# Expert results added straight into the output, and two loads and sums moved, in a four-layer graph and expert kernel

## The chip, the core and the metric

The kernel runs on one core of one Trainium2 chip. Its engines are TensorE (PE in the profile, its weight loads PEld), VectorE (DVE), ScalarE (ACT), GpSimd (POOL) and SyncE (SP). SP and ACT issue plain DMAs from their own queues, POOL issues those that use a list of indices. The metric is the device time of one execution in microseconds; the median of three runs stands for the kernel.

## The reference, cut to what matters

Input is x (625 x 1024, float32), 20,625 edges sorted by destination, with a type from 0 to 7. Four layers follow, each on the layer norm of x and added to x.

```python
# layer 1: relational graph convolution with a gate
out = x @ root + bias
for r in range(8):
    mask = (edge_type == r)
    mean = segment_sum(x[src] * mask, dst) / max(count, 1)
    out = out + mean @ weight[r]
z = concat([out, x]) @ w_gate + b_gate
h = tanh(out) * z + x * (1 - z)
# layer 2: 8-bit quantized linear layer
# layer 3: graph convolution with degree norms
# layer 4: top-2 of 8 experts, capacity 196 tokens each
combine, dispatch = _top2_gating(x @ router_w, capacity)
expert_in = einsum('nec,nh->ech', dispatch, x)
hmid = silu(einsum('ech,ehf->ecf', expert_in, w1) + b1)
expert_out = einsum('ecf,efh->ech', hmid, w2) + b2
y = einsum('nec,ech->nh', combine, expert_out)
out = y + 0.1 * (silu(x @ sw1 + sb1) @ sw2 + sb2)
```

The kernel's output is x plus the last `out`.

## The kernel before

625 rows are five tiles of 125 (`NT`). A matmul writes a PSUM tile of up to 128 x 512; four such tiles rotate (`mm_tile`). The function is built as one long program. A planner of the framework puts the instructions into each engine's queue, by its own estimate of when they can run and by the order in which they are written; at run time an engine takes its queue strictly in order. The helper `behind` asks the planner for an order without a wait, `after` adds a real wait, `in_order` chains DMAs of SP's queue, and `in_steps` and `on_pe` chain steps on TensorE.

**Units (to about 639 us).** For each relation r, `unit` (L530) multiplies the normed x with the relation's 1024 x 1024 weight, by a seven-product scheme on pairs of tiles (`tile_pair`, L452). Each recombination on VectorE is kept in `posted`; the last three of the last pair are L476, L478 and L480. Results (`ys`) go to DRAM (`yd`), except those of relation 7, which stay. Meanwhile the edges are counted in a table of DRAM (L365, L389): entry (relation, source, destination).

**Relations (about 639 to 837 us).** `order` (L580) is relation 7, then 0 to 6; I call the steps relation 0 to 7 of this stage. Each multiplies the count matrix with the unit's rows (`products`, L626), in two column halves h of five tiles t each, and adds the mean into X (L684). For exactness in the fast float format every row tile is split (`split`, L595) into an upper part `hi`, cast by ACT (L602), and the rest, by VectorE (L606). The split for the next half is written inside the loop of the present one. Also in the loop: `over_sources` (L609) sums counts over sources (L614, L616), needed by `number` (L638); `over_relations` (L619) sums counts over relations into `btot`, by an ACT copy (L622) for the first relation and VectorE additions (L624) for the rest. The area of `btot` still serves the last products of the units until they are done. Row tiles are loaded about one relation ahead (`load_y`), counts three ahead. At step `R - 3`, relation 5, SP also gets the four blocks of 1 MB of the gate's weights (L670), that `gate` reads after the loop.

**Layers 2 and 3** follow (`quantized`, `columns`, `neighbours`).

**Experts (from about 1070 us).** The router's masks give each expert a list of slots. `fill_slots` (L1155) makes `token_i`, the row of `tokens` to gather for each slot; an empty slot points to a spare row behind the 625. For the last `NL` = 4 experts there is a second list, `out_i`: in an empty slot it has a token that isn't the expert's, so that a row of zeros is added there and no spare row is needed. It comes from one-hot tiles that `find_others` (L1181, VectorE) writes and `fill_others` (L1192, TensorE) multiplies with digits of the token's number. `shared_out` (L1222) makes x + 0.1 shared in X and sends it to `total`, a DRAM area of 625 rows and the spare ones.

For expert e, `gather` brings the rows, `turn` transposes them, `expert_hidden` and `expert_out` do the two products. VectorE scales by the gate and adds the bias (L1329) into one of two `ye` buffers, and POOL adds the rows into DRAM (L1339). These scatters wait for all scatters of the expert before (`earlier`), since two experts can have a token in common. Experts 0 to 3 add to `total`. Then one DMA copies `total` to `out`:

```python
d = in_order(nc.sync.dma_start(flat_rows(out), flat_rows(total)))
after(d, [*sent, *done])
sent = [d]
```

Experts 4 to 7 add to `out`, expert 7 in halves of a row (`half_i`). The function is also written a second time, for graphs with more edges between two nodes than the fast format can hold; it is skipped here, and `exact` and `done` concern it.

Of the kernel before, what the change touches and what calls it, by code (L numbers as in the profile page):

```python
# [11 lines left out]
I32 = mybir.dt.int32  # L12
# [20 lines left out]
BEFORE = 4096.0  # L33
YB = 4 * NT
NE = 8
NL = 4
F = 256
CAP = 196
CP = CAP // 2
# [8 lines left out]
def layers(  # L48
# [163 lines left out]


    tokens = dram.tile([N + 2 * CP, D], F32, name="tokens")
    total = dram.tile([N + 2 * CP, D], F32, name="total")
    key_rows = dram.tile([ET, P], F32, name="key_rows")


# [13 lines left out]

    pe_last = None
    posted = []
    copied = []
    group = []
    counting = iter(())

# [13 lines left out]
    def weight_block(w, i, h):  # L252
        return w_chunk(wts, w, 4 * i, h * HC)
# [198 lines left out]
    def tile_pair(b, ts, put, p, between=()):  # L452
        t0, t1 = PAIRS[p]
        s1, s2, s4 = (sums[:, 3 * p + i] for i in range(3))
        steps = iter(between)

        def product(lhs, rhs):
            ps = mm_tile()
            on_pe(quarter, ps, lhs, rhs)
            for f in next(steps, ()):  # L460
                f()
            go_on()
            return ps[:P, :]
# [3 lines left out]
        copied.append(nc.scalar.copy(p1, ps))  # L467
# [12 lines left out]
        post(nc.vector.tensor_add(put(t0, 1), ps, u2))  # L480
# [98 lines left out]

    order = [R - 1, *range(R - 1)]  # L580
    counted, over, parts = {}, {}, {}

    def load_counts(r):
        counted[r] = bp.tile([P, NT, N], FR, tag="b", name="b")
# [10 lines left out]
    def split(r, h, k):  # L595

        y = held[r][k, h].bitcast(F32)
        if exact:
            parts[r, h, k] = [y]
            return  # L600
        hi = hp.tile([P, HC], F32R, tag="hi", name="hi")
        nc.scalar.copy(hi, y)  # L602
        lo = held[r][k, h]
        if r == order[0]:
            lo = yp.tile([P, HC], F32R, tag="y", name="y")
        nc.vector.tensor_sub(lo, y, hi.bitcast(F32))  # L606
        parts[r, h, k] = [lo, hi]

    def over_sources(r, k):  # L609

        v = counted[r].bitcast(F32)
        if k == 1:
            over[r] = crp.tile([P, N], FR, tag="over", name="over")
            d = nc.vector.tensor_add(over[r], v[:, 0, :], v[:, 1, :])  # L614
        else:
            d = nc.vector.tensor_add(over[r], over[r].bitcast(F32), v[:, k, :])  # L616
        behind(d, posted[-1])

    def over_relations(r, k):  # L619
        v = counted[r].bitcast(F32)[:, k, :]  # L620
        if r == order[0]:
            behind(nc.scalar.copy(btot[:, k, :], v), copied[-1])  # L622
        else:
            behind(nc.vector.tensor_add(btot[:, k, :], btot[:, k, :], v), posted[-1])  # L624

# [39 lines left out]
    firsts = [NT - 1, *range(NT - 1)]  # L665
    for k in firsts:
        split(order[0], 0, k)
    for n, r in enumerate(order):
        if n == R - 3:
            gate_w = [[weight_block(w_gate, i, h) for i in range(2)] for h in range(2)]  # L670
        for h in range(2):
            hs = slice(h * HC, (h + 1) * HC)
            for t in range(NT):
                ps = mm_tile()
# [271 lines left out]
    cleared = []  # L946
    for v in (tokens, total):
        for j in range(2):
            cleared.append(nc.scalar.dma_start(v[N + j * CP : N + (j + 1) * CP, :], zrow))

    def iota(t, pattern, base, channel):
        nc.gpsimd.iota(  # L952
# [118 lines left out]
    nc.vector.reciprocal(red, red)  # L1071
    nc.vector.tensor_mul(gates, gates, wide(red))

    NM = 2 * NE + NL
    both = mp.tile([P, NT, NM], BF16, name="masks")
    masks = both[:, :, : 2 * NE].rearrange("p t (i e) -> p t i e", i=2)
    others = both[:, :, 2 * NE :]
# [16 lines left out]
    nc.vector.tensor_add(others, masks[:, :, 0, NE - NL :], masks[:, :, 1, NE - NL :])  # L1094
    nc.vector.tensor_scalar(others, others, -1.0, 1.0, op0=ALU.mult, op1=ALU.add)


# [74 lines left out]


    aT_flat = cp.tile([P, NT * N], F32, tag="aT", name="aT")
    spots = aT_flat[:, : NL * NT * CAP // 2].bitcast(BF16)
    spots = spots.rearrange("p (e t c) -> p e t c", e=NL, t=NT)
    before = mp.tile([P, NT, NL], F32, name="before")
    out_i = mp.tile([CP, 2, NL], I32, name="out_i")
    half_i = mp.tile([CP, 2, 2], I32, name="half_i")

    def find_others():  # L1181

        nc.vector.tensor_scalar(before, others, -float(N), float(N), op0=ALU.mult, op1=ALU.add)
        nc.vector.tensor_add(before, before, pos_all[:, :NT, 2 * NE :])
        for e in range(NL):
            for t in range(NT):
                d = nc.vector.tensor_scalar(  # L1187
                    spots[:, e, t, :], io_cap, before[:, t, e : e + 1], None, op0=ALU.is_equal
                )
                behind(d, numbered[-1])  # L1190

    def fill_others(_):  # L1192
        ps = ps_sm.tile([128, HC], F32, tag="sm", name="others")
        ps = ps[:CP, : 4 * NL].rearrange("p (j e v) -> p j e v", j=2, e=NL)
        for j in range(2):
            for e in range(NL):
                for t in range(NT):
                    last = nc.tensor.matmul(
                        ps[:, j, e, :],
                        spots[:, e, t, j * CP : (j + 1) * CP],  # L1200
                        digits[:, t, :],
                        start=(t == 0),
                        stop=(t == NT - 1),
                    )
        rest_of = mp.tile([CP, 2, NL], F32, name="rest_of")
        taken_of = slots[:, :, NE - NL :, 0]
        nc.vector.tensor_scalar(rest_of, ps[:, :, :, 0], float(P), None, op0=ALU.mult)
        nc.vector.tensor_add(rest_of, rest_of, ps[:, :, :, 1])
        nc.vector.tensor_scalar(out_i, taken_of, -1.0, 1.0, op0=ALU.mult, op1=ALU.add)
        nc.vector.tensor_mul(rest_of, rest_of, out_i)  # L1210
        nc.vector.tensor_add(out_i, rest_of, slots[:, :, NE - NL :, 1])
        for h in range(2):
            nc.vector.tensor_scalar(
                half_i[:, h, :], out_i[:, :, NL - 1], 2.0, float(h), op0=ALU.mult, op1=ALU.add
            )
# [4 lines left out]
    base = []  # L1220

    def shared_out(t):  # L1222
        for h in range(2):
# [26 lines left out]
        "he": [th_flats[-1][:, c : c + 2 * CAP].rearrange("p (f c) -> p f c", f=2) for c in (0, HC)],  # L1250
    }

    def rows_at(j, e, direct=False):
        at = out_i[:, j, e - NE + NL :][:, :1] if direct else token_i[:, j, e : e + 1]
        return bass.IndirectOffsetOnAxis(ap=at, axis=0)

    def flat_rows(v):
        return v[:N, :].rearrange("n d -> (n d)").rearrange("(a b) -> a b", a=80)

    weights = {}  # L1260

# [14 lines left out]
    def gather(e):  # L1276
        for j in range(2):
            nc.gpsimd.indirect_dma_start(  # L1278
                out=rows_of_slots(e, j), out_offset=None, in_=tokens, in_offset=rows_at(j, e)
            )  # L1280

    def rows_of_slots(e, j):
        return th[2 * (e % 2) + j][:CP, :]
# [19 lines left out]
            )  # L1303
        return last

    done = sent
    sent = base + cleared

    def expert_out(e):
        nonlocal sent  # L1310
# [3 lines left out]
        for j in range(2):  # L1314
# [3 lines left out]
            for h in range(2):  # L1318
# [35 lines left out]
    for e in range(NE):  # L1354
        if 0 < e and e + 3 < NE:
            load_weights(e + 3)
        if e == 0:
            for n in range(4, NE):
                load_bias(n)
        if e == NE - NL:  # L1360
            for n in range(e + 4, NE):
                load_weights(n)
            d = in_order(nc.sync.dma_start(flat_rows(out), flat_rows(total)))
# [64 lines left out]
```

## Time and profile before

| what | before |
|---|---|
| three runs, median | 1249.19 us (1244.48 to 1249.48) |
| profiled execution, its own time | 1246.61 us |
| its span, first to last instruction | 1244.9 us |
| PE busy | 1188.5 us, 95% |
| VectorE busy | 837.9 us, 67% |
| ACT busy | 172.2 us, 14% |
| POOL busy | 487.0 us, 39% |
| mean granted TensorE clock | 0.985 |
| DMA moved | 181.72 MB, mean 146 GB/s |

The profile is of one execution. Its page gives busy times, a timeline of 40 slices, and the costliest groups of instructions with what they waited for. The trace behind it can be asked for single instructions in order of time, for who waited for whom, for the busy time of every engine in chosen stretches, and for DMA traffic. In a timeline line the columns are start, length, engine, source line, operation, output and inputs, shape and count; in brackets stand the idle time before and what released it. A line with a count above one merges instructions that follow one another. 0.3 us or less of idle time before an instruction is its issue.

### The profile page before, as it was taken

Reading aid. Unit: us, or ns where it says so; the run is one execution under the profiler, and the core shown is the slowest. Engines: PE = TensorE matmul, PEld = TensorE weight load, DVE = VectorE, ACT = ScalarE, POOL = GpSimd, SP = SyncE. Lnnn points to the kernel's source line nnn. Section 1 sums busy time; section 2 is a strip of 40 time slices with the busy share of each in tenths; the row PEclk is TensorE's granted clock in tenths of the full one; section 3 lists DMA queues with packets and bytes.
Section 4 is the critical chain, followed back from the end, with each engine's and each line's share of the span. In section 5 each row is a group of like instructions: output and inputs, shape, how many; then the busy total and the mean of one; then the engine's idle time right before and its main releaser. Section 6 shows DMA issues by size and latency. Waiting matters only on the chain. (4 is left out here: it accounts for less than half of the span.)

```text
span 1244.9 us, 11083 instructions
## 1 busy us (share of the span) xinstructions
PE 1188.5 (95%) x3810; PEld 649.8 (52%) x3810; DVE 837.9 (67%) x1340; ACT 172.2 (14%) x308; POOL 487.0 (39%) x227
## 2 busy tenths in 40 slices
PE   5999999999999999999999999899999999999992
PEld 2444444444444444444448887685445447756661
DVE  6879888888888888865149778755979416452210
ACT  1100000000000000000022122113321111313330
POOL 1005787888787888888500000004210000043312
PEclk9999999999999999999989999999999999999996
DMA  9995737373636364535455667606430025279964
GB/s 263 267 255 131 200 65 198 66 198 70 194 75 188 81 183 87 146 78 142 76 142 156 168 161 198 216 1 167 118 136 16 17 84 177 79 223 279 278 186 71
DMA packets 156288, 181.72 MB, mean 146 GB/s; under 512 B 78513, under 2 KB 95272, under 8 KB 156160
## 3 DMA queue, kind: packets, MB, share of 16 engines
q1 hardware_dynamic: 66162, 134.84, 36.7%
q0 software_dynamic: 72992, 13.31, 10.5%
q10 hardware_dynamic: 17070, 32.78, 8.6%
q8 instruction: 32, 0.52, 0.2%
q14 instruction: 32, 0.26, 0.1%
HBM read 134.22 MB, written 48.86 MB: 147 GB/s over the span
## 5 line engine op out<-in xcount | busy, mean ns | idle before, releaser
L389 POOL DMA_INDIRECT table<-hits,idx x165 | 403.8, 2447 | 199.4 <-DMA kr<-key_rows 99.7
L431 PE MATMUL mm<-w,xT 128*125 128x512 f32 x800 | 350.9, 593 | 0.0
L365 DVE SCALAR_TENSOR_TENSOR junk<-kr,key,wm 125x1375 f32<-125x1375 f32 x165 | 271.4, 1645 | 1.1
L431 PEld LDWEIGHTS mm<-w,xT 128*125 128x125 f32 x800 | 150.2, 188 | 191.7 <-issue 189.1
L629 PE MATMUL mm<-y,b 125*125 125x512 f32 x400 | 163.0, 407 | 9.1 <-DVE y L606 6.7
L629 PE MATMUL mm<-hi,b 125*125 125x512 f32 x400 | 160.5, 401 | 0.0
L431 PE MATMUL mm<-t,btot 128*125 128x512 f32 x320 | 143.8, 592 | 0.0
L1278 POOL DMA_INDIRECT th<-tokens,token_i x16 | 21.5, 1345 | 205.0 <-DVE aT L1187 172.7
L431 PEld LDWEIGHTS mm<-t,btot 128*125 128x125 f32 x320 | 60.1, 188 | 77.3 <-issue 77.3
L684 DVE SCALAR_TENSOR_TENSOR X<-mm,rc,X 125x512 f32<-125x512 f32 x80 | 59.9, 749 | 51.5 <-PE mm L629 50.4
L952 POOL IOTA io<- 125x40 f32 x1 | 0.2, 208 | 239.3 <-PE mm L629 239.3
L629 PEld LDWEIGHTS mm<-y,b 125*125 125x125 f32 x400 | 75.9, 190 | 32.2 <-DVE y L606 11.1
L629 PEld LDWEIGHTS mm<-hi,b 125*125 125x125 f32 x400 | 76.1, 190 | 18.1
L900 PE MATMUL mm<-w,xT 128*125 128x512 f32 x160 | 70.0, 595 | 2.4 <-ACT xT L187 2.4
L431 PE MATMUL mm<-w,btot 128*125 128x512 f32 x160 | 71.9, 592 | 0.0
L431 PE MATMUL mm<-t,xT 128*125 128x512 f32 x160 | 71.9, 592 | 0.0
L746 PE MATMUL mm<-w,xT 128*125 128x512 f32 x160 | 69.3, 592 | 0.0
L602 ACT CAST hi<-y 125x512 fp32r<-125x512 f32 x80 | 43.3, 617 | 147.2 <-PE mm L629 132.4
L1322 PE MATMUL mm<-w,th 128*98 128x512 f32 x128 | 56.3, 592 | 0.0
L606 DVE TENSOR_TENSOR y<-y,hi 125x512 fp32r<-125x512 f32 x80 | 53.0, 680 | 0.7 <-ACT hi L602 0.7
L450 ACT COPY y<-mm 125x512 f32<-125x512 f32 x18 | 10.5, 586 | 302.0 <-PE mm L431 291.7
L900 PEld LDWEIGHTS mm<-w,xT 128*125 128x125 f32 x160 | 29.6, 188 | 39.7 <-issue 36.0
(219 smaller groups left out, 1165.4 us busy)
## 6 DMA issues: line engine op xcount, KB each, us to landing
w<-in_L_gnn_weight_dram SPq DMA_DIRECT2D x32, 1024.0 KB
w<-in_L_ffn_w_dram SPq DMA_DIRECT2D x16, 1024.0 KB
yd<-y ACTq DMA_DIRECT2D x70, 224.0 KB
y<-yd SPq DMA_DIRECT2D x70, 224.0 KB
table<-zero SPq DMA_DIRECT2D x4, 3054.0 KB
b<-table SPq DMA_DIRECT2D x8, 1367.2 KB
kr<-key_rows ACTq DMA_DIRECT2D x15, 601.6 KB
w<-in_L_gnn_w_gate_dram SPq DMA_DIRECT2D x8, 1024.0 KB
```

Of the source, the lines that this page charges most:

```text
L365: d = nc.vector.scalar_tensor_tensor(junk, kr, key[:, c : c + 1], wm[:, (EG - 1 - j) * P : (2 * EG - 1 - j) * P], op0=ALU.is_equal, op1=AL ...
L389: d = nc.gpsimd.indirect_dma_start(out=table, out_offset=bass.IndirectOffsetOnAxis(ap=idx[:, c : c + 1], axis=0), in_=hits[:, c : c + 1], ...
L431: last = nc.tensor.matmul(ps[:P, :], lhs[:, k], rhs[:, k], start=(start and k == 0), stop=(stop and k == 3))
L450: nc.scalar.copy(put(NT - 1, h), ps[:P, :])
L602: nc.scalar.copy(hi, y)
L606: nc.vector.tensor_sub(lo, y, hi.bitcast(F32))
L629: last = nc.tensor.matmul(ps[:P, :], counted[r][:, k, t * P : (t + 1) * P], part, start=(k == ks[0] and part is parts[r, h, k][0]), stop=( ...
L684: nc.vector.scalar_tensor_tensor(X[t][:, hs], ps[:P, :], rc[:, r, t : t + 1], X[t][:, hs], op0=ALU.mult, op1=ALU.add,)
L746: last = nc.tensor.matmul(ps[:P, :], xT[:, 4 * i + k, t * P : (t + 1) * P], gate_w[h][i][:, k, :], start=(i == 0 and k == 0), stop=(i == 1 ...
L900: last = nc.tensor.matmul(ps[:P, :], xT[:, k, t * P : (t + 1) * P], gcn_w[h][k // 4][:, k % 4, :], start=(k == 0), stop=(k == KD - 1),)
L1278: nc.gpsimd.indirect_dma_start(out=rows_of_slots(e, j), out_offset=None, in_=tokens, in_offset=rows_at(j, e))
L1322: last = nc.tensor.matmul(ps[:CP, :], he[:, f, j * CP : (j + 1) * CP], weights[e][1][:, f, hs], start=(f == 0), stop=(f == 1),)
```

## The change

Four things change.

The area `total` and its copy go. `shared_out` sends x + 0.1 shared to `out`, and every expert adds there. So all eight experts need `out_i`: the masks get eight columns in place of four (`NM`), the one-hots take 40 operations and 80 products in place of 20 and 40, and their tiles lie in two areas, `aT` for six experts and the unused end of `btot` for two. `find_others` is called for two experts after each tile of `shared_out`, and `fill_others` comes after all five tiles, where it came after the second. Two clears of spare rows go as well.

The ACT copies of counts in the first relation are placed behind the cast of the tenth upper half, where they were behind the last copy of the units. The source sums of the first relation are placed behind `posted[-3]` (L476) in place of `posted[-1]` (L480).

The gate's weights are loaded one block at the start of each half of relations 3 and 4, in place of four at the start of relation 5.

```diff
@@ counts @@
-        nc.scalar.copy(hi, y)
+        upper.append(nc.scalar.copy(hi, y))
...
-        behind(d, posted[-1])
+        behind(d, posted[-3 if r == order[0] else -1])
...
         if r == order[0]:
-            behind(nc.scalar.copy(btot[:, k, :], v), copied[-1])
+            d = nc.scalar.copy(btot[:, k, :], v)
+            if not exact:
+                behind(d, upper[2 * NT - 1])
@@ gate weights @@
+    gate_w = [[], []]
     for n, r in enumerate(order):
-        if n == R - 3:
-            gate_w = [[weight_block(w_gate, i, h) for i in range(2)] for h in range(2)]
         for h in range(2):
+            if n in (3, 4):
+                gate_w[n - 3].append(weight_block(w_gate, h, n - 3))
@@ lists @@
-    NM = 2 * NE + NL
+    NM = 3 * NE
...
+    NA = 6
...
+    spots = [one_hots(aT_flat, NA), one_hots(btot_flat[:P, 2 * NT * CAP :], NE - NA)]
...
+    def find_others(e):
+        for t in range(NT):
+            d = nc.vector.tensor_scalar(
+                spot(e)[:, t, :], io_cap, before[:, t, e : e + 1], None, op0=ALU.is_equal
+            )
+            behind(d, numbered[-1])
@@ shared_out @@
-        base.extend(spread(nc.sync, total[t * P : (t + 1) * P, :], X[t]))
+        for d in spread(nc.sync, out[t * P : (t + 1) * P, :], X[t]):
+            after(d, done)
+            base.append(d)
...
-    find_others()
-    in_steps(((shared_out, 0), (shared_out, 1), (fill_others, None), *((shared_out, t) for t in range(2, NT))))
+    nc.vector.tensor_scalar(before, others, -float(N), float(N), op0=ALU.mult, op1=ALU.add)
+    nc.vector.tensor_add(before, before, pos_all[:, :NT, 2 * NE :])
+    for t in range(NT):
+        in_steps(((shared_out, t),))
+        for e in range(2 * t, min(2 * t + 2, NE)):
+            find_others(e)
+    in_steps(((fill_others, None),))
@@ expert_out and the loop over experts @@
-                    to, at, v = total if e < NE - NL else out, rows_at(j, e, e >= NE - NL), ye[:, j, :]
+                    to, at, v = out, rows_at(j, e, out_i), ye[:, j, :]
...
-        if e == NE - NL:
-            for n in range(e + 4, NE):
-                load_weights(n)
-            d = in_order(nc.sync.dma_start(flat_rows(out), flat_rows(total)))
-            after(d, [*sent, *done])
-            sent = [d]
```

More of the change, by code (lines that the diff above doesn't have):

```diff
@@ L35 @@
 NE = 8
-NL = 4
 F = 256
@@ L214, in layers @@
     tokens = dram.tile([N + 2 * CP, D], F32, name="tokens")
-    total = dram.tile([N + 2 * CP, D], F32, name="total")
     key_rows = dram.tile([ET, P], F32, name="key_rows")
@@ L234, in layers @@
     posted = []
-    copied = []
     group = []
@@ L466, in tile_pair @@
         ps = product(block(t0, 0), b[0][0])
-        copied.append(nc.scalar.copy(p1, ps))
+        nc.scalar.copy(p1, ps)
         ps = product(s2, ts[1])
@@ L581, in layers @@
     counted, over, parts = {}, {}, {}
+    upper = []
     def load_counts(r):
@@ L945, in layers @@
     nc.gpsimd.memset(zrow, 0.0)
[L946 to L949, printed above, removed]
+    for j in range(2):
+        nc.scalar.dma_start(tokens[N + j * CP : N + (j + 1) * CP, :], zrow)
     def iota(t, pattern, base, channel):
@@ L1093, in layers @@
     argmax_mask(1, rest)
-    nc.vector.tensor_add(others, masks[:, :, 0, NE - NL :], masks[:, :, 1, NE - NL :])
+    nc.vector.tensor_add(others, masks[:, :, 0, :], masks[:, :, 1, :])
     nc.vector.tensor_scalar(others, others, -1.0, 1.0, op0=ALU.mult, op1=ALU.add)
@@ L1174, in layers, with one_hots, spot @@
     aT_flat = cp.tile([P, NT * N], F32, tag="aT", name="aT")
[L1175 to L1178, printed above, removed]
-    half_i = mp.tile([CP, 2, 2], I32, name="half_i")
[L1181 to L1190, printed above, removed]
+    NA = 6
+    def one_hots(v, n):
+        v = v[:, : n * NT * CAP // 2].bitcast(BF16)
+        return v.rearrange("p (e t c) -> p e t c", e=n, t=NT)
+    spots = [one_hots(aT_flat, NA), one_hots(btot_flat[:P, 2 * NT * CAP :], NE - NA)]
+    before = mp.tile([P, NT, NE], F32, name="before")
+    out_i = mp.tile([CP, 2, NE], I32, name="out_i")
+    half_i = mp.tile([CP, 2, 2], I32, name="half_i")
+    def spot(e):
+        return spots[0][:, e] if e < NA else spots[1][:, e - NA]
+    def find_others(e):
[4 more added lines that the diff above has]
+            behind(d, numbered[-1])
     def fill_others(_):
         ps = ps_sm.tile([128, HC], F32, tag="sm", name="others")
-        ps = ps[:CP, : 4 * NL].rearrange("p (j e v) -> p j e v", j=2, e=NL)
-        for j in range(2):
-            for e in range(NL):
+        ps = ps[:CP, : 4 * NE].rearrange("p (j e v) -> p j e v", j=2, e=NE)
+        for e in range(NE):
+            for j in range(2):
                 for t in range(NT):
@@ L1199, in fill_others @@
                         ps[:, j, e, :],
-                        spots[:, e, t, j * CP : (j + 1) * CP],
+                        spot(e)[:, t, j * CP : (j + 1) * CP],
                         digits[:, t, :],
@@ L1204, in fill_others @@
                     )
-        rest_of = mp.tile([CP, 2, NL], F32, name="rest_of")
-        taken_of = slots[:, :, NE - NL :, 0]
+        rest_of = free
         nc.vector.tensor_scalar(rest_of, ps[:, :, :, 0], float(P), None, op0=ALU.mult)
         nc.vector.tensor_add(rest_of, rest_of, ps[:, :, :, 1])
-        nc.vector.tensor_scalar(out_i, taken_of, -1.0, 1.0, op0=ALU.mult, op1=ALU.add)
+        nc.vector.tensor_scalar(out_i, slots[:, :, :, 0], -1.0, 1.0, op0=ALU.mult, op1=ALU.add)
         nc.vector.tensor_mul(rest_of, rest_of, out_i)
-        nc.vector.tensor_add(out_i, rest_of, slots[:, :, NE - NL :, 1])
+        nc.vector.tensor_add(out_i, rest_of, slots[:, :, :, 1])
         for h in range(2):
             nc.vector.tensor_scalar(
-                half_i[:, h, :], out_i[:, :, NL - 1], 2.0, float(h), op0=ALU.mult, op1=ALU.add
+                half_i[:, h, :], out_i[:, :, NE - 1], 2.0, float(h), op0=ALU.mult, op1=ALU.add
             )
@@ L1219, in layers @@
     b2_first = [work.tile([P, D], F32, tag="gx", name="gx") for _ in range(2)]
-    base = []
+    done, base = sent, []
     def shared_out(t):
@@ L1251, in layers, with rows_at @@
     }
[L1253 to L1258, printed above, removed]
+    def rows_at(j, e, i):
+        return bass.IndirectOffsetOnAxis(ap=i[:, j, e : e + 1], axis=0)
     weights = {}
@@ L1278, in gather @@
             nc.gpsimd.indirect_dma_start(
-                out=rows_of_slots(e, j), out_offset=None, in_=tokens, in_offset=rows_at(j, e)
+                out=rows_of_slots(e, j), out_offset=None, in_=tokens, in_offset=rows_at(j, e, token_i)
             )
@@ L1304, in expert_hidden @@
         return last
-    done = sent
-    sent = base + cleared
+    sent = base
     def expert_out(e):
```

## The prediction

> **What bounds the kernel now.** First the page: TensorE is busy 95% of the span and the clock is granted at full speed almost everywhere, so time can only go where TensorE waits, runs at half clock, or is finished. I then listed TensorE's waits from the timeline and looked at each. After the start there are four: 2.15 us at 640.71, then 1.25 and 0.58 at 780.64 and 781.96, 4.32 at 808.49, 2.09 at 851.61. Last, the end: TensorE's last product starts at 1221.69, the span ends at 1244.9. The waits and the timeline name the owner of that end:
>
> ```profile
> POOL out_dram L1339 <- SPq L1384: 23.1, 1, 23.1
> 1180.69 3.23 SPq L1363 DMA_DIRECT2D out_dram<-total  x1
> 1199.63 1.55 POOL L1339 DMA_INDIRECT out_dram<-aT,out_i  x1 [23.13 <-SPq L1384]
> 1211.42 1.52 POOL L1339 DMA_INDIRECT out_dram<-btot,out_i  x1 [0.30 <-issue]
> 1220.69 1.52 POOL L1339 DMA_INDIRECT out_dram<-aT,out_i  x1 [0.30 <-issue]
> 1222.33 0.75 DVE L1329 SCALAR_TENSOR_TENSOR btot<-mm,slots,xn 98x512 f32<-98x512 f32 x1 [0.91 <-PE mm L1322]
> 1229.24 1.53 POOL L1339 DMA_INDIRECT out_dram<-btot,half_i  x1 [7.03 <-DMA out_dram<-aT,out_i]
> 1234.72 1.52 POOL L1339 DMA_INDIRECT out_dram<-btot,half_i  x1 [0.30 <-issue]
> ```
>
> The copy of `total` waits for expert 3's scatters to land and goes out at 1180.69; expert 4's scatter waits for the copy until 1199.63. Each later expert waits for the one before, so expert 7, whose last rows VectorE finished at 1223.1, starts at 1229.24. (The profiler names SPq L1384; only the copy was moving data then, until about 1197.)
>
> The middle stage, by relation (columns: us, busy of PE, PEld, DVE, ACT, POOL, clock, DMA share, GB/s):
>
> ```profile
> 733.30:757.10 23.80, 23.80 (x106) 18.91 (x106) 18.26 (x28) 5.41 (x10) 0.00 (x0) 1.00 0.69 175
> 757.10:783.40 26.30, 24.46 (x107) 18.88 (x106) 20.69 (x34) 5.41 (x10) 0.00 (x0) 1.00 0.73 219
> 783.40:813.40 30.00, 25.68 (x107) 20.02 (x106) 21.59 (x35) 5.41 (x10) 0.00 (x0) 0.94 0.52 155
> ```
>
> A relation takes 23.8; the two around the 4 MB of gate weights (issued from 767.18) take 26.3 and 30.0, 8.7 too many. What happens in the worse one:
>
> ```profile
> 790.73 2.70 ACT L602 CAST hi<-y 125x512 fp32r<-125x512 f32 x5 [12.01 <-DMA y<-yd]
> ...
> 805.60 2.24 DVE L624 TENSOR_TENSOR btot<-btot,b 125x625 f32<-125x625 f32 x3
> 807.76 3.09 DVE L606 TENSOR_TENSOR y<-y,hi 125x512 fp32r<-125x512 f32 x5
> 808.49 0.50 PE L629 MATMUL mm<-y,b 125*125 125x512 f32 x1 [4.32 <-DVE y L606]
> ```
>
> The rows had landed and their upper halves were cast by 793.4, yet the lower halves (L606) stand in VectorE's queue behind the count additions of L624. It is the order in the queue, not the data, that is late. And the first relation:
>
> ```profile
> 639.21 0.80 DVE L614 TENSOR_TENSOR over<-b 125x625 fp32r<-125x625 f32 x1
> 639.93 0.68 DVE L606 TENSOR_TENSOR y<-y,hi 125x512 fp32r<-125x512 f32 x1
> 640.71 0.47 PE L629 MATMUL mm<-y,b 125*125 125x512 f32 x1 [2.15 <-issue]
> 645.00:650.00 5.00, 5.00 (x15) 4.10 (x15) 3.60 (x8) 0.00 (x0) 0.00 (x0) 0.50 0.74 240
> ```
>
> The source sums (L614, L616) alternate with the lower halves, so TensorE starts 2.15 late and is fed one pair in 1.3. The last row, from the stages, shows the granted clock at 0.50: 15 products in 5 us, where a later 5 us holds 23.
>
> **The end: straight into the output.** The copy and its wait go. Late next is TensorE's own pace: expert 6's second half is ready at 1210.87 (last L1329, 1210.12 + 0.75), so its second scatter can keep today's slot of expert 5, 1211.42 to 1212.94. Two scatters landed 5.92 and 7.03 after their issue ended (the waits before 1218.86 and 1229.24); with the mean, 6.5, expert 7 starts at 1219.4 instead of 1229.24, and its fourth piece, due at 1224.9, is ready at 1223.1. All behind it moves along: **-9.8**. Earlier experts don't hold this up: with full DMA queues expert 3 lands at 1180.7, about 9.8 after its issue, and experts 4 and 5 then have 14 us each, TensorE's pace per expert. If landing stayed near 10 to the end, the gain would be 6.
>
> **Its price, stage 1088 to 1111.** VectorE gets 20 more one-hots at 0.236 (17 took 4.02): +4.7. TensorE gets 40 more small products (40 took 1.96): +2.0. Today TensorE ends this stage at 1109.1 where the turn of expert 0 begins; without the 40 products in it, 1107.1. VectorE starts at 1089.2 and has 40 x 0.236 = 9.4 plus 20 operations of 0.64 (two took 1.28) = 12.8. One-hots fill its waits for TensorE; the last stand before the last tile's 2.6, so they are done at 1089.2 + 22.2 - 2.6 = 1108.8. TensorE does 60 of the 80 products by 1110.0 and the rest by 1111.0: +1.9; with wider masks (some ten operations, about 0.03 each), **+2.3**. No gain is possible here; if the one-hots all come last, the final 20 products wait until 1111.4: +3.4. The five index operations behind them end near 1114, and expert 0's scatter isn't issued before 1123: hidden, 9 us of cover. The base rows go to `out` with the same bytes on SP's queue, the last 0.7 later; behind them there are loads for expert 3 (from 1112.62), first read at 1153.67. Their new wait is for scatters of an earlier pass, and in this pass there is none. The bias row of expert 7 now lies where one-hots were and waits for the products, done by 1111; it is issued at 1118.43 today. Two small clears of `total` go from ACT's queue, beside a full TensorE: nothing.
>
> One rule speaks against more one-hots here. The gather of expert 0 shows it:
>
> ```profile
> 1089.59 5.20 POOL L1278 DMA_INDIRECT th<-tokens,token_i  x1 [172.66 <-DVE aT L1187]
> 1089.86 4.02 DVE L1187 TENSOR_SCALAR aT<-io_cap,before 125x196 bf16<-125x196 f32 x17
> ```
>
> It took 5.20 where later ones take about 1.0, and ended 0.9 after the one-hots. The Trainium skill ("SBUF — State Buffer", Who interferes with whom) says that a tensor_scalar in a two-port mode shuts GpSimd out for its whole length, and that GpSimd then can't write descriptors. By the rule, strictly, gather 0 could wait for all forty, until 1108.8, and with its second half (1.3) and some 3 us of flight turn expert 0 at 1113: +2 more. By the row, a gather gets in once the run of one-hots is broken, and the change breaks it with additions after each tile: it finishes by about 1103, and costs nothing. I take the row; the other end goes into the range.
>
> **Count sums earlier, count copies later.** The four source sums (0.72 apart) may now stand two posts earlier, from 633.0 on, where VectorE waits 2.15 and 2.74 for TensorE. Then L606 runs five times at 0.6 after 638.6 at the latest, not alternating: the last lower half is there at 642.4, not 646.4, and the next tile's products start at 643.4 instead of 647.41: **-4.0**. The clock is the second part. The Trainium skill ("TensorE: Matmul & The Clock Gate", HAM oscillation) puts the danger at idle gaps above about 3.4 us; here gaps of 2.15 and 0.58 were followed by the 0.50 of the row above: products 0.43 apart up to 651.8, then 0.23. By the rule nothing more is to be won; by the row a shorter gap saves up to ten products at 0.2, 2 us. I take a quarter, -0.5. **Sum -4.5**; bounds: -6.0 if the clock holds, +0.7 if a sum gets in front of the last recombination and nothing else moves. The copies of counts on ACT move behind ten casts; ACT then idles until 657, and the first reader of those sums comes later: nothing.
>
> **Gate weights one block per half.** Same 4 MB, two relations earlier, in four pieces of about 2.7 us at the 384 GB/s seen at 776 to 779. DMA is idle 5 of the 24 us of a relation, so real landing is no problem. What counts is the order in VectorE's queue. Counting in the timeline how many L684 of a half stand before the first L606 of the second-half groups, relations 1 to 6 give -1 (still in the half before), 0, 1, 2, 3, 5 (of five): the planner already holds the rows later by one tile each relation, and at 3 TensorE waited 1.83, at 5 it waited 4.32 plus half clock until 812.3 (1.7). Best: both waits go, -7.9. Worst of the plausible: blocks in front of the groups read in relations 4 to 6 push three or four groups to 4 and 5, at 2 to 4.3 each, about 13 in place of 7.9: +5. Nearest is relation 5's row, which keeps a wait of about 2, and one of some 3 for relation 6, and half the clock loss: I take **-1**.
>
> **Sum.** -9.8 + 2.3 - 4.5 - 1 = -13.0 against the profiled execution, 1246.61: 1233.6. That execution lies 2.6 below the median shown; the median gives 1236.2. I forecast **1235**.
>
> **Rivals.** (a) All queue-order stalls vanish and the clock holds: -7.5 - 6.0 - 7.9, about 1225. For it: DMA has room; against: the drift of one tile per relation, which is there before any gate block. (b) Only the end gains, the middle gives it back: -7.5 - 1 + 5, about 1243. (c) **Slower:** the early blocks put all six groups of relations 4 to 7 behind their last addition, each paying 4.32 + 1.7 = 6.0: 36 in place of 7.9, less 12 from the rest: +16, 1263. It decides from 20 us of stalls in that stage on. For it: that order is planned, and 808 shows its price; against: late groups can't all be late, since one pause moves the plan of those behind. (d) The scatters aren't freed, landing near 10 throughout: 4 less gain, 1239.
>
> **Numbers.** The likeliest case with (d) 0.53, its own range 1229 to 1241; (a) 0.19; (b) 0.18; (c) 0.10. Below 0.5% (6 us) this kernel's runs can't tell a change. Faster by over that (under 1242.9): 0.53 + 0.19 + a small part of (b), 0.75; within: 0.15; slower 0.10. Range 1224 to 1247.
>
> **What would show it.** Right: no copy and no wait of 20 us before a scatter; from TensorE's last product to the span's end some 13 us (23 today); 22 to 24 us from the first slot numbers to the turn of expert 0 (20.5 today); source sums between 633 and 639; waits of 1 to 3 us in relations 5 and 6. Wrong: expert 0's turn waiting for its gather, L606 behind L624 in relations 4 and 5, or the first products still 0.43 apart for 10 us.

## The result, and the profile after

The changed kernel takes 1252.84 us, the median of 7 runs (1251.0 to 1253.05); the kernel before, in as many runs, 1248.56 (1244.48 to 1249.82). The ratio is **1.0035**, 95% interval 1.0022 to 1.0049: some 4 us slower, just under what I had said this kernel's runs can tell from no change, and nowhere near the 1235 of the forecast. The profiled execution took 1252.84, against 1246.61 before.

The page's first rows hold no hint: TensorE is busier than before (1188.5 then), and everybody else is where they were.

```profile
span 1251.1 us, 11175 instructions
PE 1201.7 (96%) x3850; PEld 658.7 (53%) x3850; DVE 843.7 (67%) x1360; ACT 172.1 (14%) x308; POOL 487.4 (39%) x227
```

13 us more of busy TensorE, and the new small products are worth 2: a busy TensorE at half clock counts as busy. So I took the stages one by one. The **end**, from the timeline (start, length, engine, line, operation; in brackets the idle time before and its releaser):

```profile
1227.78 1.52 POOL L1344 DMA_INDIRECT out_dram<-aT,out_i  x1 [1.91 <-DVE aT L1334]
1234.84 1.53 POOL L1344 DMA_INDIRECT out_dram<-btot,half_i  x1 [5.54 <-DVE btot L1334]
...
1238.93 0.75 DVE L1334 SCALAR_TENSOR_TENSOR btot<-mm,slots,xn 98x512 f32<-98x512 f32 x1 [0.91 <-PE mm L1327]
1240.32 1.52 POOL L1344 DMA_INDIRECT out_dram<-btot,half_i  x1 [0.30 <-issue]
```

No copy and no wait of 20 us is left; the scatters of experts 5 to 7 now wait for VectorE's rows, that is for TensorE's pace. One scatter, the first of expert 4 (1196.90), still waits 3.79 for those of expert 3 to land. From TensorE's end (1238.9) to the end of the span there are 12.2 us, before there were 22.6: 10.4 won. The **first relation** won too:

```profile
638.76 4.29 DVE L604 TENSOR_TENSOR y<-y,hi 125x512 fp32r<-125x512 f32 x7
639.54 0.47 PE L629 MATMUL mm<-y,b 125*125 125x512 f32 x1 [1.85 <-issue]
```

The lower halves (L604 now) stand in one run, with no source sum between them, and the second tile's products start at 644.10, not 647.41. Both gains are eaten in the **relations**. In the windows (length; busy of PE, PEld, DVE, ACT, POOL; granted clock; DMA share; GB/s) the same kind of stretch that took 23.8, 26.3 and 30.0 before now reads:

```profile
729.50:757.60 28.10, 26.16 (x106) 19.79 (x105) 20.99 (x33) 5.41 (x10) 0.00 (x0) 0.93 0.97 264
757.60:791.20 33.60, 28.57 (x106) 21.63 (x106) 20.22 (x32) 5.41 (x10) 0.00 (x0) 0.86 0.65 167
791.20:823.90 32.70, 28.51 (x106) 21.02 (x106) 20.29 (x33) 5.41 (x10) 0.00 (x0) 0.87 0.13 40
823.90:849.20 25.30, 25.30 (x101) 20.00 (x101) 13.05 (x22) 2.70 (x5) 0.00 (x0) 0.90 0.00 1
```

Two things are lost together: TensorE idles (length less PE busy: 1.9, 5.0, 4.2) and runs below full clock. The timeline at the worst place shows why it idles:

```profile
766.43 2.70 ACT L600 CAST hi<-y 125x512 fp32r<-125x512 f32 x5 [15.24 <-PE mm L629]
...
780.36 0.74 DVE L685 SCALAR_TENSOR_TENSOR X<-mm,rc,X 125x512 f32<-125x512 f32 x1
781.02 0.80 DVE L614 TENSOR_TENSOR over<-over,b 125x625 fp32r<-125x625 f32 x1
781.74 0.80 DVE L624 TENSOR_TENSOR btot<-btot,b 125x625 f32<-125x625 f32 x1
782.46 0.80 DVE L614 TENSOR_TENSOR over<-over,b 125x625 fp32r<-125x625 f32 x1
783.18 0.80 DVE L624 TENSOR_TENSOR btot<-btot,b 125x625 f32<-125x625 f32 x1
783.89 0.69 DVE L604 TENSOR_TENSOR y<-y,hi 125x512 fp32r<-125x512 f32 x1
784.64 0.79 PE L629 MATMUL mm<-y,b 125*125 125x512 f32 x1 [4.81 <-DVE y L604]
```

All five upper halves of this group (relation 5, second half) are cast between 766.4 and 769.1, so the rows had landed. The first lower half comes at 783.89, 14.8 us after the last cast, behind the half's last addition into X (L685) and four sums of counts that nobody waits for yet. VectorE was not short of time: it stood idle for about 1.55 before each of the additions at 772.91, 775.22 and 777.53, waiting for TensorE, with the lower halves further back in its queue. It is the picture that the kernel before showed in full once, at 808.49, and mildly at 780.6. Now it stands at three places: TensorE waits 1.25 + 0.58 at 752.7, 4.81 at 784.6, and 1.93, 0.59, 0.60 and 0.96 from 815.6 on. The order in VectorE's queue can be counted: how many of the half's five additions stand before each of the five lower halves of a group.

| group for | before | after |
|---|---|---|
| relation 4, second half | 2, 3, 3, 4, 5 | 4, 4, 5, 5, 5 |
| relation 5, first half | 1, 1, 2, 3, 4 | 2, 3, 3, 4, 5 |
| relation 5, second half | 3, 4, 4, 5, 5 | 5, 5, 5, 5, 5 |
| relation 6, first half | 1, 1, 2, 3, 3 | 2, 3, 3, 4, 5 |
| relation 6, second half | 5, 5, 5, 5, 5 | 5, 5, 5, 5, 5 |

Last, the stage where the lists are made, and the turn of expert 0:

```profile
1103.14 1.73 POOL L1284 DMA_INDIRECT th<-tokens,token_i  x1 [172.61 <-DVE token_i L1168]
...
1120.72 2.87 PE L1201 MATMUL others<-digits,aT 125*98 125x2 bf16 x60
1123.46 1.05 PE L1201 MATMUL others<-digits,btot 125*98 125x2 bf16 x20
1124.38 0.87 PE L183 MATMUL tr<-ident,th 98*128 98x98 f32 x8
```

The first gather takes 1.73, where it took 5.20 before, and the turn waits for the 80 products, not for it. From the slot products to the turn it is 1.75 longer than before, and from the turn to TensorE's end 1.3, where the clock is at half from 1125.7 to 1129.1.

**Where the time went**, from milestones that both traces have (after less before): up to relation 3, -3.7 (0.5 to 0.9 of it an earlier start of the whole stage); relations 4 to 7, **+16.65**; the layers between, +0.65; lists and experts, +3.1; the end, -10.4. The sum is +6.3, the spans differ by 6.2.

### The profile page after: what moved, and what is told of

Its sections match the earlier page's. It is cut to its first block, busy times and chain, and to the rows that moved or that the text cites. A ratio compares the mean times of both kernels' runs of the same rounds, so it can differ in the third digit from the quotient of the medians.

```text
span 1251.1 us, 11175 instructions
## 1 busy us (share of the span) xinstructions
PE 1201.7 (96%) x3850; PEld 658.7 (53%) x3850; DVE 843.7 (67%) x1360; ACT 172.1 (14%) x308; POOL 487.4 (39%) x227
## 4 chain that ended last, share of the span: by engine, by line
PE 88%; DMA 3%; DVE 3%; ACT 3%; issue 1%; POOL 1%; SPq 0%; ACTq 0%; POOLq 0%; DVEq 0%
PE mm L428 49%; PE mm L629 14%; PE mm L901 6%; PE mm L1327 4%; PE mm L1300 3%; PE mm L747 3%; PE mm L929 2%; PE tr L183 2%; PE mm L1229 2%; PE mm L1015 1%; PE mm L878 1%; DMA X<-in_x_dram 1%; DMA w<-in_L_gnn_w_gate_dram 1%; DVE xn L168 1%; PE lgT L1002 1%
## 5 line engine op out<-in xcount | busy, mean ns | idle before, releaser
L386 POOL DMA_INDIRECT table<-hits,idx x165 | 408.3, 2475 | 196.3 <-DMA kr<-key_rows 98.0
L629 PE MATMUL mm<-y,b 125*125 125x512 f32 x400 | 168.0, 420 | 13.0 <-DVE y L604 10.7
L629 PE MATMUL mm<-hi,b 125*125 125x512 f32 x400 | 164.5, 411 | 0.0
L685 DVE SCALAR_TENSOR_TENSOR X<-mm,rc,X 125x512 f32<-125x512 f32 x80 | 59.9, 749 | 66.7 <-PE mm L629 65.9
L1284 POOL DMA_INDIRECT th<-tokens,token_i x16 | 17.4, 1085 | 212.7 <-DVE token_i L1168 172.6
L604 DVE TENSOR_TENSOR y<-y,hi 125x512 fp32r<-125x512 f32 x80 | 52.9, 681 | 0.7 <-ACT hi L600 0.7
```

What stands on the lines that cost most here:

```text
L386: d = nc.gpsimd.indirect_dma_start(out=table, out_offset=bass.IndirectOffsetOnAxis(ap=idx[:, c : c + 1], axis=0), in_=hits[:, c : c + 1], ...
L629: last = nc.tensor.matmul(ps[:P, :], counted[r][:, k, t * P : (t + 1) * P], part, start=(k == ks[0] and part is parts[r, h, k][0]), stop=( ...
L685: nc.vector.scalar_tensor_tensor(X[t][:, hs], ps[:P, :], rc[:, r, t : t + 1], X[t][:, hs], op0=ALU.mult, op1=ALU.add,)
```

## The experiments

My theory after this reading: the gate's blocks, moved early, put the lower halves later in VectorE's queue, by the planner's order, while the data are in time. Rivals: the loads really delay the rows (DMA is 97% busy in the first of those windows); the loss is chiefly TensorE's clock; the loss comes from the other parts of the change. In all, ten kernels were run, each with runs of the kernel before on the same chip (medians 1249.69, 1249.55 and 1247.19). Below, "us" of a ratio means its distance from 1 times 1249.

**Gate weights put back (e1).**

```diff
-    gate_w = [[], []]
     for n, r in enumerate(order):
+        if n == R - 3:
+            gate_w = [[weight_block(w_gate, i, h) for i in range(2)] for h in range(2)]
         for h in range(2):
-            if n in (3, 4):
-                gate_w[n - 3].append(weight_block(w_gate, h, n - 3))
```

> The changed kernel with the gate's weights back at the start of relation 5, four blocks at once. Theory (order): the early blocks made the planner put lower halves of relations 4 to 6 late in VectorE's queue, and that cost 16.6 us in the profiles (products of relation 3's end to the turn after relation 7: 3.7 ahead before, 12.95 behind after). Then this takes about 1236, and the waits of TensorE around relation 5 and 6 are those of the kernel before (1.25, 0.58, 4.32). Rival 1 (data): rows land late because the blocks take DMA time; it gives the same here. Rival 2 (sums): the earlier source sums upset the later queue; then this stays above 1245.

Measured: 1238.18 (1235.21 to 1242.64), ratio 0.992, interval 0.9894 to 0.9946. The queue order is that of the kernel before again, in every group of the table, and so are the waits (1.25 and 0.59 in relation 5, then):

```profile
802.28 2.24 DVE L624 TENSOR_TENSOR btot<-btot,b 125x625 f32<-125x625 f32 x3
804.45 1.89 DVE L604 TENSOR_TENSOR y<-y,hi 125x512 fp32r<-125x512 f32 x3
...
805.18 0.74 PE L629 MATMUL mm<-y,b 125*125 125x512 f32 x1 [4.32 <-DVE y L604]
```

That is the 4.32 of the kernel before, to the hundredth. Changed kernel over this one: 1.0035 / 0.992, about 14.4 us for the gate's move.

**Blocks stay early, order held by hand (e2).** Every addition into X is asked to stand behind a lower half, with no wait added:

```diff
+        lower.append(nc.vector.tensor_sub(lo, y, hi.bitcast(F32)))
...
-                nc.vector.scalar_tensor_tensor(
+                d = nc.vector.scalar_tensor_tensor(
...
+                if n > 1 and t > 0 and not exact:
+                    behind(d, lower[-1])
```

> The changed kernel, gate blocks early as they are, but from relation 2 on each addition L685 is held behind the lower half written before it, an order within VectorE's queue and no wait. DMAs and their place in SP's queue stay. Order: TensorE's long waits go, the queue has 1, 2, 3, 4, 5 additions before the five lower halves of a group, and the time is 1229 to 1236. Data: the additions now wait for late rows too, so nothing is won and the time is 1250 or more.

Measured: 1235.13 (1234.3 to 1236.13), ratio 0.9881, interval 0.9862 to 0.9901. The loads are where the changed kernel has them, DMA is 94% busy in the stretch of relation 4, and most of the loss is gone:

```profile
728.60:754.70 26.10, 24.81 (x107) 19.12 (x107) 20.69 (x33) 5.41 (x10) 0.00 (x0) 1.00 0.94 255
754.70:782.10 27.40, 26.08 (x107) 19.98 (x106) 19.89 (x33) 5.41 (x10) 0.00 (x0) 0.94 0.85 230
782.10:807.40 25.30, 25.30 (x106) 20.07 (x105) 17.87 (x29) 5.41 (x10) 0.00 (x0) 0.94 0.19 58
```

That is 26.1, 27.4 and 25.3 in place of 28.1, 33.6 and 32.7. So it was the order. The rows are not late: in all five groups of the table the last upper half was cast 4.5 to 7.9 us before the first lower half began (9.1 to 15.2 in the changed kernel). Of the waits of about 0.5 that are left, the profile puts two down to a row's load (at 751.98 and 779.38), but the casts of these groups had ended by 738.9 and 766.2; each of these products starts when its own lower half is done.

**Blocks behind the last row load (e3), and the same with the order held (e4).**

```diff
                 load_y(order[n + 1 + h], 1 - h)
+            if (n, h) == (R - 2, 0):
+                gate_w = [[weight_block(w_gate, i, g) for i in range(2)] for g in range(2)]
```

> The changed kernel with the four gate blocks behind the last row load, in relation 6. Order: no rows are behind the blocks, and groups of relations 5 and 6 stand at 3, 4, 4, 5, 5; two waits of about 1.8 remain and no long one, so about 4 us under e1: 1232. Rival 2 (sums): above 1245. A cost of its own: if the blocks land after relation 7, the gate stage waits, and the time is above e1.

> e3 with the order of e2. Order: the two waits of 1.8 shrink to about 1 or less; 1229 to 1231. If VectorE, not the order, is the limit in these relations, e3 and e4 agree within 1 us.

Measured, e3: 1237.63 (1236.08 to 1239.01), ratio 0.9907 (0.9886 to 0.9929), no better than e1. The wait of 4.32 did go; in its place there are two small ones, which the timeline of TensorE shows:

```profile
803.59 0.49 PE L629 MATMUL mm<-y,b 125*125 125x512 f32 x1 [1.25 <-DVE y L604]
...
804.91 0.55 PE L629 MATMUL mm<-y,b 125*125 125x512 f32 x1 [0.59 <-DVE y L604]
```

After this pair the clock was at half for 6.8 us, from 805.2; the same pair in the kernel before, at 780.6, cost no clock at all. That is part of what my figure of 1232 lacked. What it costs can be read where the order is the same: from the first product of relation 5's second half to that of relation 6's the kernel before and e1 take 30.8 each, with full clock after the pair; e6 and e7 take 33.9 and 33.8, with 6.8 us at half clock after it. That is 3.1 us.

e4: **1227.96** (1227.54 to 1229.57), ratio **0.9825**, interval 0.9806 to 0.9844. Its windows are what the stage looks like with nothing in the way: TensorE busy for the whole length, full clock, three equal relations.

```profile
733.00:757.00 24.00, 24.00 (x107) 19.08 (x106) 18.69 (x30) 5.41 (x10) 0.00 (x0) 1.00 0.66 173
757.00:781.00 24.00, 24.00 (x107) 19.05 (x107) 19.87 (x32) 5.41 (x10) 0.00 (x0) 1.00 0.69 173
781.00:805.00 24.00, 24.00 (x107) 19.05 (x106) 19.85 (x31) 5.41 (x10) 0.00 (x0) 1.00 0.65 229
```

It is the fastest of all: 1.75% under the kernel before, somewhat lower than the 1229 to 1231 that I had expected. It is also 7.2 us under e2, so with the order held by hand it still matters where the loads stand: in e2 eight sums of counts stand in front of the first lower half of the second-half groups of relations 4 and 5, in e4 four.

**One part each, on the kernel before (e5, e6, e7).** The diffs are those of the change: e5 has only the gate's blocks, e6 only the straight adding, e7 only the sums and copies of counts.

> The kernel before with the gate blocks alone moved (one at the start of each half of relations 3 and 4). Order: the cost doesn't need the other parts; the groups of relations 4 to 6 stand as late as in the changed kernel (first lower half after 4, 2, 5, 2, 5 additions), and the time is 1249 + 15 to 17, about 1265. Rival 2 (the sums upset it): below 1255.

> The kernel before with the straight adding alone. From the profiles, the end gains 10.4 and the stage ahead of the experts loses 2 to 3: 1241 to 1242. If the gain of the end needs an earlier middle, 1246 or more.

> The kernel before with the source sums earlier and the count copies later, alone. From the profiles, the first relation gains 3.0 to 3.7: 1245 to 1246. If those 3.7 were only an earlier start of the run, 1249.

| part alone | median (range) | ratio (interval) | us |
|---|---|---|---|
| e5, gate blocks | 1263.01 (1260.93 to 1264.05) | 1.0101 (1.0067 to 1.0136) | +12.6 |
| e6, straight adding | 1242.55 (1238.97 to 1246.79) | 0.9943 (0.9923 to 0.9963) | -7.1 |
| e7, sums and copies | 1243.84 (1240.28 to 1246.9) | 0.9959 (0.9945 to 0.9973) | -5.1 |

The three add up to +0.4, the whole measured +4.4; with the widths of the intervals (4.3, 2.5 and 1.7 us to each side) that is no contradiction. e5 has the queue order of the changed kernel in all five rows of the table of groups above, and its windows, three microseconds later, are nearly a copy (28.1, 33.9 and 32.7 long, clock 0.94, 0.85 and 0.87). So the loss needs neither of the other parts. In e6 the price of the straight adding is seen by itself: slot products to TensorE's end 140.2 against 137.4 before, +2.8.

**The middle of e4 on the kernel before (e8).** It asks whether the gain of e4 needs the straight adding and the count sums.

> The kernel before with the middle of e4 (gate blocks behind the last rows, additions held behind lower halves), without the straight adding and without the moved sums. It has no stalls in relations 4 to 6 left: 7.9 us under the kernel before, 1241. Against e4 it shows what the two good parts are worth where nothing else moves: 10 to 13 us more than e4.

Measured: 1239.22 (1235.89 to 1240.92), ratio 0.9903 (0.9867 to 0.994). A clean middle is worth about 12 us to the kernel before by the ratio (7.5 to 16.6; 10.3 by the medians), more than the 7.9 that I had read from its profile, and the other two parts 0.9825 / 0.9903, 9.9 us by the ratios and 11.3 by the medians, on top. Gains from different stages add within these widths: 12.1, 7.1 and 5.1 make 24.3, and e4 has 21.9.

**Is it the clock? (e9)** On the changed kernel, extra products whose result nobody reads fill TensorE's waits in relations 4 and 5:

```diff
         for k in ks:
+            for _ in range(idle[k] if idle else 0):
+                nc.tensor.matmul(
+                    spare[:P, :], counted[r][:, k, :P], parts[r, h, k][-1], start=True, stop=True
+                )
...
+                idle = {4: (2, 2, 3, 3, 3), 5: (20, 3, 3, 2, 2)}.get(n, ())
```

> The changed kernel, gate blocks early as they are, with 43 extra products whose result nobody reads, at the first tile of the second half of relations 4 and 5, where TensorE waits for lower halves: they keep it busy and change no order up to there. If the half clock is most of the loss (27 us at half clock after the change, 3.4 before), the stretch from relation 3's end to the first tile of relation 5's second half, 61.8 us in the changed kernel, shrinks by 5 to 8 us though more work is done. If the waits themselves are the loss, it stays or grows by up to 2. In the whole, 1244 to 1249 against 1253.

```profile
729.50:757.60 28.10, 28.10 (x124) 21.95 (x123) 20.81 (x33) 5.41 (x10) 0.00 (x0) 1.00 0.95 264
757.60:790.00 32.40, 32.24 (x141) 25.15 (x140) 21.23 (x33) 5.41 (x10) 0.00 (x0) 1.00 0.68 174
```

The clock is whole (1.00, where it was 0.93 and 0.86). Yet the two relations, from the second tile of relation 3's second half to that of relation 5's, shrink only from 61.75 to 58.70, by 3.05; I had expected 5 to 8. TensorE at full speed gains little there, since it still goes by the lower halves: in relation 5 the late tile's first three pairs start at 782.01, 783.33 and 784.65, each 0.05 to 0.1 after its lower half is done, 1.32 apart, just as in the changed kernel (784.64, 785.96, 787.28); the full pace is 0.47. Only from the fourth pair on do the extra products themselves hold the kernel's own back, by some 0.9, so that up to 4 may be the clock's. By either figure it is the smaller part of the 13.9 that these two relations lose against e4. The kernel as a whole ran 1242.38 (ratio 0.9965, 0.9953 to 0.9976), but with the extra products the planner also put relation 6's groups earlier (6, first half: 1, 1, 2, 3, 3; second half: 3, 4, 4, 5, 5), so it can't be set against the changed kernel. It can be set against e10 below, which has the same order in all five groups.

**Two blocks early, two late (e10).**

```diff
-            if n in (3, 4):
-                gate_w[n - 3].append(weight_block(w_gate, h, n - 3))
+            if n == 3:
+                gate_w[0].append(weight_block(w_gate, h, 0))
...
+            if (n, h) == (R - 2, 0):
+                gate_w[1] = [weight_block(w_gate, i, 1) for i in range(2)]
```

> The changed kernel with only the first two gate blocks early (relation 3), the other two behind the last row load. Order: VectorE's queue now has the groups of relation 4 and the second of 5 as late as in the changed kernel, the later ones back at 1 and 3 additions, so half to two thirds of the 16.6 us remain: 1246 to 1249. If the number of early bytes doesn't matter, only that there are any: 1252. If only relation 6 mattered: 1238.

Measured: 1244.88 (1243.0 to 1249.88), ratio 0.9987 (0.9974 to 1.0001). Over e1 that is 0.67%, 8.4 us: 58% of what all four blocks cost, the share expected; the time is a little below the 1246 to 1249 expected, as the kernel before, run beside it, was lower too (1247.19). In the queue, relation 4's second half and both halves of relation 5 have the changed kernel's order, and relation 6 does not (its first half 1, 1, 2, 3, 3, its second 3, 4, 4, 5, 5): the two blocks that were left early keep their damage, the two that were moved took theirs along.

With the order the same, e9 and e10 differ in the extra products and the clock. From the second tile of relation 3's second half to relation 7's first product, e10 takes 99.4 us, 17.1 of them at half clock; e9 takes 94.3, all at full clock, and e4, with a clean order, 81.1. So the half clock cost some 5 us there and the order itself some 13. (The whole kernels differ by 2.5: 1244.88 and 1242.38.) At this rate, 0.3 us for each us at half clock, the 27.3 us of the changed kernel against the 3.4 of the kernel before make some 7 of the 16.65 us; that is an estimate. The clock is thus no small part of the loss, but it comes with the order: where the order is clean (e4, e8) there is no half clock in these relations.

## Why the prediction was wrong

**The step that failed is the gate's weights.** The prediction read the right place. It saw that real landing was no problem (though DMA is idle for 7 to 8 of the 24 us of a relation, by its share of 0.65 to 0.69, and not for 5), that "what counts is the order in VectorE's queue", that the groups slip by about an addition with each relation, and what a group behind the last addition costs. Then it said: "Nearest is relation 5's row, which keeps a wait of about 2, and one of some 3 for relation 6, and half the clock loss: I take -1." Measured: +12.6 alone, +14.4 on top of the other two parts, +16.65 between the two profiles. (The profile gives most since the kernel before was profiled in one of its faster executions.) The step treated the move as a reshuffle, with relation 5 as it was and relation 6 a little better. That the blocks add to the slip stood only in its worst case and in rival (c), and was weighed at nothing in the -1. They do add to it: relation 4's second half went from 2 additions ahead to 4, relation 5's from 3 to 5, and relation 6's, at 5 already, kept its place. The waits followed the count much as the rows of the trace before had said they would: 3 gave 1.83 before, and 4 gives the same 1.83 now; 5 gave 4.32 before, 4.81 and 4.08 now. Even the "worst of the plausible", +5, was under the truth, because it priced 2 to 4.3 for a late group and left out two things: the slow pace after the wait (with a sum of counts between every two lower halves the pairs come 1.32 apart in place of 0.47, at full clock too, e9), and the half clock, 27.3 us in place of 3.4.

**The rival that came closest in mechanism was (c), the slower one** (in the number, (b) with 1243 and (c) with 1263 miss by about as much). Its mechanism is the one that the runs show: early blocks put groups behind the last addition. Its size was too large, +28 in that stage, since only two second-half groups stood behind all five additions, and one had stood there before; the first halves took no harm (2, 3, 3, 4, 5 cost no wait). I argued against it that "one pause moves the plan of those behind"; the table shows no such relief. That all this comes from the planner's estimate of when rows land is inferred: the estimate itself appears in no trace. Shown is that the order changes with the blocks and with nothing else in the change (e1, e5, e10), that the rows are there (the casts at 766.4, e2), and that holding the order wins the loss back with the loads left early (e2).

The **end** was right: -10.4 for -9.8, and 12.2 us left where 13 were forecast. The link was another one, though: the forecast let expert 7 start when expert 6's rows have landed, 6.5 after their issue. Here it starts 5.54 after it, with VectorE's rows, and only expert 4's first scatter waits for another. That the number is so close is in part luck. Rival (d) falls: expert 3's rows took 9.7 to land, expert 6's at most 5.5. The **price** was right in kind and a little small: +3.1 for +2.3. From the first slot numbers to the turn it is 22.3 (22 to 24 forecast); up to the turn it cost 1.75; what was missing is the half clock after the 80 products, 1.3. Of the rule and the row that were weighed there, the row holds: the gather took 1.73 and finished long before the one-hots did. (The section cited there speaks of the length of one instruction; that the gather waits for all forty was my strict reading of it.) The first run of one-hots was five long here (to 1103.95), and the gather ended 0.92 behind it, as it ended 0.9 behind the long run before; a rule by which it waits for all forty, the last of which ended at 1123.3, would have put it 18 us later. Gather and run go together in all twelve profiles: 5.20 behind a run of twenty in the four with twenty one-hots, 1.72 or 1.73 behind one of five in the eight with forty, and an end about 0.9 behind the run. Alone, the part gave -7.1, for -7.5.

The **count sums** were right: -5.1 (-6.9 to -3.4) alone, for -4.5. The first tile's products did not start much earlier (the wait is 1.85, it was 2.15), but the second tile starts at 644.1, where I had 643.4. Of the 3.7 in the profiles 0.5 to 0.9 is an earlier start of the stage, not a gain of the sums. The half clock there lasted 6.8 us, 10.2 before; over all profiles it is 10.2 in the four kernels with the sums where they were, and 0, 3.4 or 6.8 in the eight with them earlier. Pauses well under the 3.4 of the rule cost clock again, so there too the row spoke truer than the rule.

Together: end -0.6, price +0.8, sums +0.8, layers between +0.65 against the forecast's terms, and the gate +17.65. These make up the 19.2 us (rounding aside) between -13.0 and +6.2; 92% of it is one term.

## What to carry to other kernels

Where a planner places instructions by its own estimate of when data land, moving a load early can make its neighbours' consumers late although no data are: count, in the queue of the engine between load and matmul, how many other operations stand ahead of each consumer, and price the change by what it adds to that count. If a trace already shows the count growing from stage to stage, expect a load put in front to make it grow faster, as here; hold the order by hand first (here e2, e4), then measure where the load stands best (e4 and e2 are 7.2 us apart). And measure each part of a combined change alone: two good parts worth 10 to 12 us were hidden here under a third.

## What the hardware showed that I had not expected

- **A dense run of tiny products was followed by half clock.** The 80 products of two columns fill TensorE for 3.9 us (see 1120.72 above), and the turn follows. In all eight profiled kernels that have them the granted clock then fell to half, at 1102.7 to 1125.7, for 3.4 us (6.8 in e6). In the four without the straight adding the same turn, behind full products, has full clock. The 40 slot products of 24 columns, 3.6 us, were followed by 3.4 us at half clock in nine of the twelve kernels (at 1088.8 in the kernel before), the 40 products of two columns of the four, 2.0 us, in none. What in such a run does it was not tried apart. The row of the changed kernel:

```profile
1125.00:1130.00 5.00, 4.76 (x23) 4.35 (x22) 1.56 (x8) 1.80 (x4) 1.97 (x2) 0.66 1.08 347
```

- **The same pause does not always cost the same clock.** Waits of 1.25 and 0.58, 1.3 apart, were followed by full clock in the kernel before and in e1, and by 6.8 us at half clock in e6 and in e7; in e3 the first such pair (777.3) cost none and the second (803.6) 6.8. The pause of about 2 us before the first relation was followed by nothing, 3.4, 6.8 or 10.2 us of half clock, by kernel. What decides was not tried; a clock loss of this size should go into a range, not into a sum.
